# The opening of a one-core convolution and scan kernel: load order, the bias of the output, and the request for the second step's input

## The chip, the core and the metric

The kernel runs on one NeuronCore of a Trainium2 chip. The metric is the time of one execution on the device in microseconds; lower is better. PE is the matmul engine, PEld its weight loads, DVE the vector engine, ACT the scalar engine, POOL GpSimd, and SP the engine that issues nearly all DMAs. SBUF is the on-chip memory, PSUM the accumulator memory of PE with eight banks.

## The reference

The input x has the shape (4, 128, 96, 96) in fp32. Each image is normalised in 32 groups of four channels, and read as four sequences of 9216 positions: by rows, by columns, and both backwards. Each sequence goes through one block, and the four results are joined by one more matrix:

```python
t = grouped1x1(gn(x), in_proj_w, in_proj_b, 4)        # 128 -> 512 channels
u, gate = t[:, :256], t[:, 256:]
u = depthwise_conv5(silu(u), dw_w)
s, a = ssm_in(u), 0.999 + 0.0009 * sigmoid(delta(u))
h = linear_scan(a, tanh(b(u)) * s)                    # h[l] = a[l] h[l-1] + b[l] s[l]
u = u + ssm_out(tanh(c(u)) * h + d * s)
y_dir = out_proj(grouped1x1(u * sigmoid(gate), mix_w, mix_b, 4))
out = x + fuse_w @ concat(y_1 .. y_4) + fuse_b
```

`out_proj`, `mix` and `fuse` are linear with nothing between them. They can be multiplied into one matrix for each direction, `w_fin`, and one bias, `b_fin`, which is the same for all positions: the sum over the four directions d of `fuse_d (out_proj mix_b + out_proj_b)`, plus `fuse_b`.

## The kernel before

A sequence is cut into steps of 1536 positions (16 lines of the image). A position has one of R = 4 residues modulo four, so a step holds 4 x 384 positions; a *pair* is one step at one residue, for two sequences (s = 0 and s = 1) at once. For each pair the kernel runs, in this order: the *front* (`in_proj` from `x_in`, then `silu`), the depthwise convolution (half of the channels on PE as `conv` and `conv_less`, half as five taps, the first on ACT in L649 and four on DVE in L651, the last of which writes `u`), the projections `proj`, the scan, and, six pairs later, the gate, the output matmuls and the sum into `acc`. `pair(t)` computes the front of pair t + 4. Order on every engine is written out by hand from `start()` on; the opening before it is ordered by the framework's scheduler. In both kernels each engine runs its own instructions in order.

The opening has two threads.

- **Statistics.** `load_x` brings the whole first image into `acc` (4.7 MB, eight DMAs, one to four chunks of 384 positions each) and DVE runs one `bn_stats` for each of 24 chunks (L282). `stats_finish` then makes the normalised input weights `wn` and their bias `bnorm`: L184 on DVE, a small matmul L187 on PE, DVE, L199 on PE, DVE and ACT, L226 on DVE (which reads `main`), L235 on PE.
- **Weights.** `small`, `fuse` and `main` are loaded by ACT (L275). From `fuse`, PE makes `w_of` (eight matmuls, L364) and from that the final weights (eight, L371), with ACT copying each result. Twelve one-column matmuls (L379) add up the bias. Then `stay_busy` (L286) runs matmuls whose results nobody uses: four of 512 columns at once, and one of 256 and one of 512 columns inside the statistics' chain.

SP issues the loads of x, then the first step's `x_in` (L253) and gate inputs (L268). The program has eight semaphores for these DMAs in rotation, so that a DMA is issued only when the one eight before it has landed.

`start()` then runs the four residues of step 0: `burst(0, g)` (the matmuls for the first 32 of each sequence's 64 own rows of `x_in`), the silus of them, `burst(1, g)` for the second 32 rows, and after each of those `after_front(0, g)`, which asks for the next step's x: rows 64s+32 to 64s+64 of residue g each time, and rows 64s to 64s+32 of all residues when g is 3. Those rows may be overwritten once their bursts have read them. `pair(0)` follows. Its `proj` calls the front of step 1 (`front(4)`) between its own two halves; the first half reads `u` of the convolution on PE, the second `u` of the taps. `front(4)` uses PSUM banks 5, 4, 2 and 3, and `conv(2)` of the next pair uses 4 and 5. L632 and L634 are ACT's copies of the convolution's result into `u`; L683, L684 and L689 are ACT's reads of `proj`.

```python
def after_front(step, g):
    for s in range(2):
        load_front(step + 1, s, slice(64 * s + 32, 64 * s + 64), slice(g, g + 1))
    if g == R - 1:
        for s in range(2):
            load_front(step + 1, s, slice(64 * s, 64 * s + 32), slice(0, R))
```

Of the kernel before, what the change touches and what calls it, by code (L numbers as in the profile page):

```python
# [50 lines left out]
HID, MH, K = 256, 32, 5  # L51
# [5 lines left out]
R = 4  # L57
# [10 lines left out]
def conv_preact_kernel(  # L68
# [9 lines left out]
    nc = tc.nc  # L78

    wp = ctx.enter_context(tc.tile_pool(name="weights", bufs=1))  # L80
# [48 lines left out]
    def bank(i):  # L129
        return psum[:, i, :]  # L130

    def mm(o, col, lhsT, rhs, start, stop):
        r = slice(32 * col, 32 * col + 32)
        nc.tensor.matmul(o[r, : rhs.shape[-1]], lhsT, rhs, start=start, stop=stop,  # L134
                         skip_group_check=True)
# [35 lines left out]
    def stats_of(b):  # L171
        if b not in stats:
            stats[b] = sp.tile([P, NSC, 6], F32, tag="bn", name=f"bn_{b}")
        return stats[b]
# [71 lines left out]
    def fresh(step):  # L246

        return step * UB < NU and step % NS < NS // 2

    def load_front(step, s, r, q):  # L250
        if fresh(step):
            un = units[step * UB + s]
            nc.sync.dma_start(  # L253
                x_in[s][r, q, :], xs[un["b"], un["lay"], r, q, bass.ds(un["st"] * N, N + 1)]
            )
# [14 lines left out]
                xs[un["b"], un["lay"], half(1 - un["s"]), q, bass.ds(un["st"] * N, N + 1)],  # L270
            )

    def load(src, name, pool=wp):
        t = pool.tile(list(src.shape), F32, tag=name, name=name)
        nc.scalar.dma_start(t, src)  # L275
        return t

    def load_x(chunks):
        for c, n in chunks:
            nc.sync.dma_start(accf[:, bass.ds(c * SC, n * SC)], xr[b0, :, bass.ds(c * SC, n * SC)])  # L280
            for e in range(c, c + n):
                nc.vector.bn_stats(stats_of(b0)[:, e, :], accf[:, bass.ts(e, SC)])  # L282

    def stay_busy(n):
        if n:
            nc.tensor.matmul(  # L286
                bank(free[0] ^ 1)[:, :n], w_fin[:, 0, 0, :],
                w_fin.rearrange("p d j c -> p (d j c)")[:, :n], start=True, stop=True,
                skip_group_check=True,
            )  # L290
# [8 lines left out]
    pp = prep.__enter__()  # L299
    load_x([(0, 1), (1, 2), (3, 3)])  # L300
    w_small = load(small, "small")
    load_x([(6, 4)])
    w_out_fuse = load(fuse, "fuse", pp)
    load_x([(10, 4)])
    w_main = load(main, "main")
    load_x([(14, 4), (18, 4), (22, 2)])
    for s in range(2):
        load_front(0, s, half(s), slice(0, R))
    for i in range(UB):
# [4 lines left out]
    d_sb, b_mix, b_out, b_fuse = (w_small[:, a:b] for a, b in ((79, 80), (80, 82), (82, 83), (83, 84)))  # L314
    w_out = w_out_fuse[:, 0:HID]
    w_fuse = w_out_fuse[:, HID : HID + 4 * P].rearrange("p (d c) -> p d c", d=4)
    w_mix = w_out_fuse[:, HID + 4 * P :].rearrange("p (j c) -> p j c", j=2)
    w_in, w_proj = (
        w_main[:, bass.ts(e, HID)].rearrange("p (j c) -> p j c", j=2) for e in range(2)
    )  # L320
    w_so = w_main[:, bass.ts(2, HID)]

    nc.vector.tensor_scalar_mul(b_proj[64:P, 0:1], b_proj[64:P, 0:1], 0.5)
    nc.vector.tensor_scalar_mul(
        w_proj[:, :, 2 * MH : 3 * MH], w_proj[:, :, 2 * MH : 3 * MH], 0.5
    )


    def less_of(p):
# [30 lines left out]
    w_of = pp.tile([P, 4, 2, P], F32, name="w_of")  # L360
# [12 lines left out]
            )  # L373
            nc.scalar.mul(w_fin[:, d, j, :], pt[:, :P], 0.5)
    pb = bank(0)
    terms = [(w_of[:, d, j, :], b_mix[:, j : j + 1]) for d in range(4) for j in range(2)]
    terms += [(w_fuse[:, d, :], b_out) for d in range(4)]
    for i, (lhsT, rhs) in enumerate(terms):
        nc.tensor.matmul(  # L379
            pb[:, 0:1], lhsT, rhs, start=(i == 0), stop=(i == len(terms) - 1)  # L380
        )
    nc.scalar.activation(b_fin, pb[:, 0:1], AF.Identity, bias=b_fuse)
    for _ in range(4):
        stay_busy(512)
    prep.__exit__(None, None, None)

    wk = ctx.enter_context(tc.tile_pool(name="work", bufs=2))
# [64 lines left out]
    def edges(step, g, j, engine):  # L452
        sil = sils[step]
        if j == 0:
            for s in range(2):
                engine.memset(sil[64 * s : 64 * s + 64, s, 0, g, 0:1], 0.0)
        elif g < 2:
            engine.memset(sil[:, :, 1, g, 0:1], 0.0)

    def after_front(step, g):  # L460
        for s in range(2):
            load_front(step + 1, s, slice(64 * s + 32, 64 * s + 64), slice(g, g + 1))
        if g == R - 1:
            for s in range(2):
                load_front(step + 1, s, slice(64 * s, 64 * s + 32), slice(0, R))
        if step % NS < NS // 2 - 1:
            to_keep.append((step, g))
        if step > 1:
            keep_silu(1)
# [3 lines left out]
    def keep_silu(n):  # L473
        for step, g in to_keep[:n]:
            nc.sync.dma_start(kept_sil[step // NS % 2][step % NS][g], sils[step][:, :, :, g, :])
        del to_keep[:n]
# [9 lines left out]
    def in_proj(step, g, s, j, bk):  # L486
        wn = stats[units[step * UB]["b"]][0]
        r = slice(64 * s + 32 * j, 64 * s + 32 * j + 32)
        for c in range(4):
            m, q = (c, g) if j else (g, R - 1 - c if s else c)  # L490
            mm(bank(bk), c, wn[r, s, 32 * m : 32 * m + 32], x_in[s][r, q, :], True, True)

    def silu(step, g, s, j, bk):
        bn = stats[units[step * UB]["b"]][1]
        nc.scalar.activation(  # L495
            sils[step][:, s, j, g, :],
            bank(bk)[:, : N + 1],
            AF.Silu,
            bias=bn[:, 1:2] if j else bn[:, 4 + g : 5 + g],
        )  # L500
# [112 lines left out]
    def conv(i, banks):  # L613

        step, p = units[i]["step"], units[i]["p"]
        sil, k, b0 = blocks(step), less_of(p), min(banks)
        for s in range(2):
            for g in range(4):
                mm(bank(b0 + s), g, band[:, s, p, g, :], columns(step, sil[s][:, g, :], 1 - k),
                   True, False)  # L620

    def conv_less(i, banks):
        step, p = units[i]["step"], units[i]["p"]
        sil, k, b0 = blocks(step), less_of(p), min(banks)
        for g in range(4):
            for s in range(2):
                r = less_rows(s, p)
                mm(bank(b0 + s), g, less[r, p, g, :], columns(step, sil[s][r, g, :], k),
                   False, True)
        if banks == PROJ:  # L630
            for s in range(2):
                nc.scalar.copy(us[i][:, s, 0, :], bank(b0 + s)[:, :N])  # L632
        else:
            nc.scalar.copy(us[i][:, :, 0, :], psum[:, b0 : b0 + 2, :N])  # L634

    def new_u(i):
        us[i] = wk.tile([P, 2, 2, N], F32, tag="u", bufs=LAG + 2, name=f"u_{units[i]['id']}")

    def taps(i, ks):

        un = units[i]
        step = un["step"]
        sil = sils[step][:, :, 1] if fresh(step) else sils[step][:, ::-1, 1, ::-1]
        part = psum[:, TAPS : TAPS + 2, :N]
        for k in ks:
            off, q = divmod(un["p"] + k, R)
            src = columns(step, sil[:, :, q, :], off)
            if k == 0:
                nc.scalar.activation(part, src, AF.Copy, scale=w_tap[:, 0:1])  # L649
            else:  # L650
                nc.vector.scalar_tensor_tensor(  # L651
                    us[i][:, :, 1, :] if k == K - 1 else part,
                    src,
                    w_tap[:, k : k + 1],
                    part,
                    ALU.mult,
                    ALU.add,
                )
# [130 lines left out]
    def head_banks(t):  # L789

        return PROJ if t % 2 or t >= LAG else FRONT[1::-1]
# [209 lines left out]
    def start():  # L1001
        pieces = stats_finish(b0)
        for wait in (0, 256, 512, 0, 0):
            next(pieces, None)
            stay_busy(wait)
        sils[0] = wk.tile([P, 2, 2, 4, N + 1], F32, tag="sil", name="sil_0")
        banks = ((2, 3), (4, 5), (6, 7), (0, 1)), ((2, 3), (4, 5), (2, 3), (4, 5))

        def burst(j, g):
            for s in range(2):  # L1010
                in_proj(0, g, s, j, banks[j][g][s])

        def silus(j, g):
            for s in range(2):
                silu(0, g, s, j, banks[j][g][s])
            edges(0, g, j, nc.vector)

        for g in range(R):
            burst(0, g)
        for g in range(R):  # L1020
            silus(0, g)
        new_u(0)
        for g in range(R):
            burst(1, g)
            silus(1, g)
            after_front(0, g)
            if g < 2:
                taps(0, (g,))
            if g == 1:
                conv(0, head_banks(0))  # L1030
                conv_less(0, head_banks(0))
        taps(0, (2, 3, 4))
# [89 lines left out]
```

## Time and profile before

| what | value |
|---|---|
| three runs | 1831.49, 1835.07 and 1840.69 us; median 1835.07 |
| the profiled execution | 1833.3 us, of which the span of its instructions is 1831.6 us |
| granted PE clock, mean of the span | 0.996 |
| PE busy | 1806.8 us (99%) |
| ACT, DVE, POOL busy | 1566.0 us (86%), 1448.8 us (79%), 1423.5 us (78%) |
| DMA | 321 MB, 175 GB/s on average |

The profile gives the start and the length of each instruction, what ended the idle time before it, and the landing of each DMA; times are counted from the start of the span. A matmul in fp32 stands in it as two passes, each a record, so that eight matmuls are "x16".

### The profile page before, as it was taken

What the parts mean: (1) busy time and instruction counts of PE and PEld (TensorE: products, weight loads), DVE (VectorE), ACT (ScalarE), POOL (GpSimd) and SP (SyncE); (2) the same over time, 40 slices, a digit from 0 to 9 for tenths busy, and PEclk for the clock granted to TensorE, in tenths of its full rate; (3) what the DMA queues carried; (4) which work ended last, traced back from release to release, by engine and by line L of the source; (5) the groups of instructions that cost most, each with busy time, mean ns of one, the idle gap of its engine ahead of it and who ended that gap; (6) DMA issues with size and microseconds to landing.
All of it is one profiled execution on the core that took longest, in us unless ns stands there. A gap on an engine that the chain in (4) does not pass through costs nothing.

```text
span 1831.6 us, 57282 instructions
## 1 busy us (share of the span) xinstructions
PE 1806.8 (99%) x24068; PEld 653.9 (36%) x24068; DVE 1448.8 (79%) x1451; ACT 1566.0 (86%) x2762; POOL 1423.5 (78%) x1469
## 2 busy tenths in 40 slices
PE   7999999999999999999999999999999999999998
PEld 4333333333333333333333333333333333333333
DVE  5888878877878888877778888877877778777886
ACT  4888888988888888888898888888888888888975
POOL 2487887778777888787877888787877788887785
PEclk8999999999999999999999999999999999999999
DMA  6755563444965566244696546443476634535434
GB/s 196 200 191 179 164 192 108 161 144 147 307 227 181 167 188 190 102 142 140 214 296 207 165 162 211 136 152 110 162 236 223 234 123 152 192 109 179 148 122 156
DMA packets 147825, 321.18 MB, mean 175 GB/s; under 512 B 14192, under 2 KB 115696, under 8 KB 147568
## 3 DMA queue, kind: packets, MB, share of 16 engines
q1 hardware_dynamic: 147136, 316.56, 53.1%
q8 instruction: 190, 3.11, 0.7%
q10 hardware_dynamic: 432, 0.96, 0.1%
q14 instruction: 67, 0.55, 0.1%
HBM read 185.21 MB, written 132.25 MB: 173 GB/s over the span
## 4 chain that ended last, share of the span: by engine, by line
PE 96%; ACT 2%; DMA 1%; DVE 1%; issue 0%; SPq 0%; POOL 0%; ACTq 0%; DVEq 0%; POOLq 0%
PE psum L134 82%; PE psum L520 8%; PE psum L514 5%; ACT sil L495 0%; DMA x_in<-in_xs 0%; DMA fuse<-in_fuse 0%; PE psum L286 0%; DVE u L600 0%; ACT t L701 0%; ACT t L689 0%; PE psum L364 0%; ACT psum L649 0%; DMA out<-acc 0%; ACT u L632 0%; DVE psum L651 0%
## 5 line engine op out<-in xcount | busy, mean ns | idle before, releaser
L651 DVE SCALAR_TENSOR_TENSOR psum<-sil,small,psum 128x768 f32<-128x768 f32 x576 | 588.9, 1022 | 33.2 <-ACT psum L649 7.4
L600 DVE SCALAR_TENSOR_TENSOR u<-gate,psum 128x768 f32<-128x768 f32 x376 | 349.6, 952 | 256.6 <-ACT gate L537 118.6
L134 PE MATMUL psum<-u,w_fin 128*32 128x384 f32 x6176 | 551.7, 487 | 0.2 <-ACT t L689 0.2
L134 PE MATMUL psum<-u,main 128*32 128x384 f32 x6144 | 536.4, 490 | 0.1
L770 POOL TENSOR_TENSOR acc<-ys,acc 128x384 f32<-128x384 f32 x374 | 412.2, 1122 | 33.3 <-ACT ys L751 9.1
L724 POOL TENSOR_TENSOR t<-t,t 64x384 f32<-64x384 f32 x191 | 234.9, 1230 | 158.4 <-PE psum L514 78.8
L134 PEld LDWEIGHTS psum<-u,w_fin 128*32 128x32 f32 x6176 | 189.1, 110 | 320.8 <-issue 218.7
L134 PEld LDWEIGHTS psum<-u,main 128*32 128x32 f32 x6144 | 181.6, 110 | 327.6 <-issue 199.1
L528 ACT COPY psum<-u 128x768 f32<-128x768 f32 x352 | 276.9, 800 | 20.7 <-DVE u L651 10.2
L691 POOL TENSOR_SCALAR t<-tm 64x384 f32<-64x384 f32 x191 | 177.0, 927 | 151.0 <-ACT tm L683 100.8
L134 PE MATMUL psum<-sil,band 128*32 128x384 f32 x3072 | 286.8, 489 | 3.1 <-ACT ys L753 3.1
L725 POOL TENSOR_TENSOR t<-t,t 64x384 f32<-64x384 f32 x191 | 246.4, 1290 | 15.0
L520 PE MATMUL psum<-t,main 32*128 32x384 f32 x1536 | 241.9, 513 | 3.3 <-ACT psum L528 2.6
L649 ACT ACTIVATE psum<-sil,small 128x768 f32<-128x768 f32 x192 | 174.1, 907 | 63.2 <-DVE u L600 53.7
L537 ACT ACTIVATE gate<-psum,bnorm 128x384 f32<-128x384 f32 x384 | 192.6, 582 | 28.9 <-PE psum L514 26.9
L692 POOL TENSOR_TENSOR t<-t,tm 64x384 f32<-64x384 f32 x192 | 195.0, 1016 | 15.4 <-ACT t L684 0.2
L651 DVE SCALAR_TENSOR_TENSOR u<-sil,small,psum 128x768 f32<-128x768 f32 x192 | 194.9, 1015 | 7.8
L495 ACT ACTIVATE sil<-psum,bnorm 128x385 f32<-128x385 f32 x384 | 191.7, 584 | 3.6 <-PE psum L134 1.4
L134 PE MATMUL psum<-sil,less 64*32 64x384 f32 x3072 | 168.2, 495 | 0.0
L514 PE MATMUL psum<-x_in,wn 32*128 32x384 f32 x768 | 162.0, 528 | 2.3 <-ACT u L632 1.2
L753 ACT COPY ys<-psum 128x384 f32<-128x384 f32 x281 | 129.9, 476 | 30.2 <-PE psum L134 29.2
L134 PEld LDWEIGHTS psum<-sil,band 128*32 128x32 f32 x3072 | 90.2, 109 | 175.6 <-issue 94.1
(92 smaller groups left out, 1500.3 us busy)
## 6 DMA issues: line engine op xcount, KB each, us to landing
sil<-sil SPq DMA_DIRECT2D x128, 770.0 KB, 6.7
kept<-gate SPq DMA_DIRECT2D x80, 768.0 KB, 3.7
gate<-kept SPq DMA_DIRECT2D x76, 768.0 KB, 5.2
x_in<-in_xs SPq DMA_DIRECT2D x192, 96.2 KB, 2.4
out<-acc SPq DMA_DIRECT2D x48, 384.0 KB, 8.0
acc<-in_xr SPq DMA_DIRECT2D x38, 384.0 KB, 6.9
xs<-in_xr SPq DMA_DIRECT2D x72, 192.0 KB, 4.7
x_in<-in_xs SPq DMA_DIRECT2D x184, 48.1 KB, 3.7
```

Of the source, the lines that this page charges most:

```text
L134: nc.tensor.matmul(o[r, : rhs.shape[-1]], lhsT, rhs, start=start, stop=stop, skip_group_check=True)
L495: nc.scalar.activation(sils[step][:, s, j, g, :], bank(bk)[:, : N + 1], AF.Silu, bias=bn[:, 1:2] if j else bn[:, 4 + g : 5 + g],)
L514: nc.tensor.matmul(bank(to)[:, :N], stats[un["b"]][0][r, s, :], x_in[s][r, q, off : off + N], start=True, stop=True)
L520: nc.tensor.matmul(bank(SSM + 2 * s + j)[:, :N], w_so[r, bass.ts(j, P)], z[r, :], start=bi not in seeded, stop=True, skip_group_check=True)
L528: nc.scalar.copy(psum[:, SSM + 2 * s : SSM + 2 * s + 2, :N], us[bi][:, s])
L537: nc.scalar.activation(gv[:, s, j, :], bank(to[2 * s + j])[:, :N], AF.Tanh, bias=bn[:, 2 + j : 3 + j], scale=0.5,)
L600: nc.vector.scalar_tensor_tensor(v, g, 1.0, pz, ALU.add, ALU.mult)
L651: nc.vector.scalar_tensor_tensor(us[i][:, :, 1, :] if k == K - 1 else part, src, w_tap[:, k : k + 1], part, ALU.mult, ALU.add,)
L692: nc.gpsimd.tensor_mul(ta[0:64, p, :], tb[0:64, :], tm[0:64, :])
L724: engine.tensor_mul(ta[0:64, p, :], tb[64:P, :], ta[64:P, p, :])
L725: engine.tensor_add(tb[0:64, :], ta[0:64, p, :], tb[0:64, :])
L770: adder.tensor_add(part, y, part)
```

## The change

It touches the opening alone, in five places.

1. `fuse` and `main` are loaded by SP and no longer by ACT: `fuse` behind the first ten chunks of x, `main` behind all of them.
2. The halving of a part of `w_proj` moves from the head of the program to a place in `start()` behind the statistics' chain. It is on DVE in both.
3. The bias of the output takes three matmuls: `w_of` and `w_fuse` are first summed over the four directions, by four adds on POOL that write into their first slices.
4. The four 512-column `stay_busy` matmuls ahead of the statistics' chain are left out.
5. For step 0, the rows 64s to 64s+32 of the next step's x are asked for right behind the four `burst(0, g)`, and no longer behind the last `after_front(0, 3)`. The later steps are as before.

```diff
-    def load(src, name, pool=wp):
+    def load(src, name, pool=wp, queue=nc.scalar):
         t = pool.tile(list(src.shape), F32, tag=name, name=name)
-        nc.scalar.dma_start(t, src)
+        queue.dma_start(t, src)
         return t
...
     load_x([(6, 4)])
-    w_out_fuse = load(fuse, "fuse", pp)
-    load_x([(10, 4)])
-    w_main = load(main, "main")
-    load_x([(14, 4), (18, 4), (22, 2)])
+    w_out_fuse = load(fuse, "fuse", pp, nc.sync)
+    load_x([(10, 4), (14, 4), (18, 4), (22, 2)])
+    w_main = load(main, "main", wp, nc.sync)
...
-    nc.vector.tensor_scalar_mul(
-        w_proj[:, :, 2 * MH : 3 * MH], w_proj[:, :, 2 * MH : 3 * MH], 0.5
-    )
...
     pb = bank(0)
-    terms = [(w_of[:, d, j, :], b_mix[:, j : j + 1]) for d in range(4) for j in range(2)]
-    terms += [(w_fuse[:, d, :], b_out) for d in range(4)]
+    for w in (w_of, w_fuse):
+        for e in (2, 1):
+            nc.gpsimd.tensor_add(w[:, 0:e], w[:, 0:e], w[:, e : 2 * e])
+    terms = [(w_of[:, 0, j, :], b_mix[:, j : j + 1]) for j in range(2)]
+    terms += [(w_fuse[:, 0, :], b_out)]
...
     nc.scalar.activation(b_fin, pb[:, 0:1], AF.Identity, bias=b_fuse)
-    for _ in range(4):
-        stay_busy(512)
...
-        if g == R - 1:
+        if g == R - 1 and step:
             for s in range(2):
                 load_front(step + 1, s, slice(64 * s, 64 * s + 32), slice(0, R))
...
         for wait in (0, 256, 512, 0, 0):
             next(pieces, None)
             stay_busy(wait)
+        nc.vector.tensor_scalar_mul(
+            w_proj[:, :, 2 * MH : 3 * MH], w_proj[:, :, 2 * MH : 3 * MH], 0.5
+        )
...
         for g in range(R):
             burst(0, g)
+        for s in range(2):
+            load_front(1, s, slice(64 * s, 64 * s + 32), slice(0, R))
         for g in range(R):
             silus(0, g)
```

## The prediction, made before the changed kernel ran

> **What bounds the kernel now.** I read the page first: PE is busy for 1806.8 us of a span of 1831.6 us, so nearly all of the time that an edit of the opening could give back lies where PE is not yet running without breaks. Then I read the chain of waits for the first 120 us, the timeline of the same stretch, and the busy time in windows of 2 us. The chain (start, length, what):
>
> ```profile
> 1.31 5.42 DMA fuse<-in_fuse
> ...
> 13.42 2.57 PE psum L379 x24
> 16.00 5.24 PE psum L286 x8
> 21.24 0.13 PE psum L187 x2
> ...
> 33.74 3.40 DMA x_in<-in_xs
> 37.14 0.14 issue
> 37.28 7.77 PE psum L134 x80
> 45.05 0.05 ACT u L632
> ```
>
> Two places stand out. Ahead of 21.24 the chain lies on filler matmuls (L286), not on data. At 33.74 it lies on the load of the second step's x. The timeline says how near the next limit is in the first place:
>
> ```profile
> 10.87 8.52 DVE L282 BATCH_NORM_STATS2 bn<-acc 128x6 f32<-128x384 f32 x18 [0.25 <-DMA acc<-in_xr]
> 15.86 5.38 PE L286 MATMUL psum<-w_fin 128*128 128x512 f32 x8
> 19.42 0.80 DVE L184 BATCH_NORM_AGGREGATE mv<-bn 128x2 f32<-128x144 f32 x1
> 21.07 0.28 PE L187 MATMUL psum<-mv,gmean 128*128 128x1 f32 x2
> ```
>
> DVE has the means ready at 20.22 (19.42 + 0.80), but PE comes to L187 only at 21.07: the fillers cost 0.85 us, and DVE with the arrival of x sets the rest. In the second place:
>
> ```profile
> 36.00 1.01 DVE L651 SCALAR_TENSOR_TENSOR u<-sil,small,psum 128x768 f32<-128x768 f32 x1
> 37.11 0.91 ACT L649 ACTIVATE psum<-sil,small 128x768 f32<-128x768 f32 x1 [2.38 <-DVE u L651]
> 38.84 2.00 ACT L495 ACTIVATE sil<-psum,bnorm 128x385 f32<-128x385 f32 x4 [0.83 <-PE psum L134]
> 41.22 1.01 DVE L651 SCALAR_TENSOR_TENSOR u<-sil,small,psum 128x768 f32<-128x768 f32 x1
> ```
>
> So x at 37.28 is a wait for PE, but ACT could not have started the second step's silus before 38.02 anyway (L649 stands ahead of them and waits for DVE). The windows show what the gap did besides (length, PE, weight loads, DVE, ACT, POOL, granted clock, DMA):
>
> ```profile
> 34.00:36.00 2.00, 0.47 (x8) 0.00 (x0) 1.86 (x3) 0.73 (x2) 0.00 (x0) 1.00 0.49 126
> 36.00:38.00 2.00, 0.72 (x24) 0.36 (x32) 1.01 (x1) 0.89 (x1) 0.00 (x0) 0.65 0.41 113
> 38.00:40.00 2.00, 2.00 (x36) 0.33 (x24) 1.92 (x2) 1.17 (x4) 0.00 (x0) 0.50 0.06 13
> 40.00:42.00 2.00, 2.00 (x20) 0.66 (x16) 1.93 (x3) 1.42 (x3) 0.32 (x1) 0.50 0.57 179
> ```
>
> The clock fell to half and stayed there until 43.41 (clock records of the trace), so PE paid double from 37.28 on.
>
> **What the skill says.** TensorE: Matmul & The Clock Gate, section "What's actually happening": the array runs at half clock until it has been busy for a free-running window of about 3.4 us and falls back after an idle one. The trace agrees: a 512-column pass takes 0.85 us before 19.52 and 0.43 after, and the records change at steps of 3.413 us (16.105, 19.519, 36.585, 43.412). DMA: Bandwidth & Descriptors, "Issuing engines are not separate DMA queues": loads issued by ACT and SP share the same engines. The trace agrees: fuse (ACT) and the second x chunk (SP) land together at 6.74 and 6.24, and the pipe keeps some 418 GB/s with one issuer or two. GPSIMD Engine Reference, "Elementwise — side-by-side cycle accounting": 2.6 cycles an element for a two-input add; the rows here (128x128 0.40 us, 128x384 about 1.1) are what I use.
>
> **Part 1, order of the loads.** From 10.84 to 16.50, 2.36 MB of x landed, 417 GB/s; cumulative bytes B then land at about 3.82 us + B/417. With x ahead of main, and fuse behind the first ten chunks, I get: x chunks 0–9 by 3.5, 5.3, 6.8 and 8.6 (before 3.53, 6.24, 8.84, 10.84); fuse 9.9 (before 6.74); then 11.8, 13.7, 15.6, 16.5 (before 12.74, 14.61, 16.50, 18.11); main 17.4 to 18.1. A DMA waits for the landing of the one eight before it; the eight ahead of each land at least 1 us before the pipe needs it, so I put this at nothing. x_in comes behind the same bytes, so it lands as before, 19.94 and 21.88. DVE takes 0.473 us a chunk: it now waits for chunk 10 until 11.8 and is then level with the pipe (1.89 against 1.88 us for four), so six chunks after 15.55 end at 18.45: 0.94 us earlier, which is main's 0.39 MB. Bounds 0.4 and 1.4. ACT issues two DMAs fewer, at no gain: it idles until 7.61. The half scaling of w_proj (0.36 us of DVE) moves behind L240, where DVE waits 0.99 us for a silu: nothing, and 0.36 us if that cover is gone. main is needed at L226, some 22 us: 4 us of cover.
>
> **Part 2, bias from three matmuls.** 24 passes of 0.112 us (2.57) become 6 (0.7 at full clock, 1.3 at half). POOL gets four adds, estimated from its rows at 2.5 ns an element: 0.72, 0.39, 1.35, 0.72. fuse lands at 9.9, L364 and L371 take 16 passes of 0.213 us each at half clock, to 16.9. The w_fuse adds run from 13.5; the w_of adds from 15.3, when the first half of L371 is done, to 17.4; bias 18.1 to 18.8. The means are ready at 18.45 + 0.83 = 19.28. It is hidden, with a cover of 0.5 to 1.2 us; without it (second half of L371 awaited, adds at double) L187 moves to 20.4, a loss of 1.1.
>
> **Part 3, four fillers gone.** L187 starts at 19.3 in place of 21.07: 1.75 us, part 1 included. Against it stands the clock, which the fillers raised at 19.52. PE now has a hole from about 17 to 19.3, shorter than a window. If the clock stays high, the first burst starts at 22.6 (24.33 before); x_in at 21.88 allows it. If it is low, the 512-column filler kept behind L199 takes 1.71 us and ends at about 23.0, so that L235 gains 0.75, the bursts start at 24.0, and a group takes 0.64 us against ACT's 0.48 per silu until the clock rises, one window later on average: in sum 0 to 0.3 gained. I take the mean of the two, 1.0 us; bounds -0.6 and +1.75.
>
> **Part 4, the second step's x.** Two issues of 0.64 us move on SP ahead of eight smaller ones (0.37 each). Their wait for PE ends with the first bursts, near 26.9, so it holds nobody back; the first of the eight, at 27.37, slips to about 28.2 and lands at 30, wanted at 34.5. The load lands near 31 instead of 37.14, after the last of the first bursts. In the times of before, with the burst's own shift apart: front(4)'s matmuls run from 34.75, when silu has freed banks 4 and 5, to 36.1; proj's second half waits for u until 37.05 (before 39.37); ACT's L649 stays at 37.11, silus 38.04 (before 38.84), tm, L684 and L689 end at 41.5 (before 43.3). conv(2) waits for banks 4 and 5, freed by the second silu at 39.0, and runs at full clock 39.05–40.35, conv_less to 41.1 (before 44.9). Next is the copy L632: 41.5 against 45.03, **3.5 us**; then L649 and the taps follow, as u (42.23) is done. If the clock falls all the same, conv_less ends at 43.0, 2.0 us. The window from 33.17 to 36.58 was busy for 1.3 us of 3.41 when the clock fell; with front(4) in it, it is for 2.6. So I count the high clock two to one, and take 3.0. Late next are DVE's taps and ACT. From 57.48 the third step's load has its old place and moves with the rest (PE waits 0.5 there). PE has no break after about 80 us, so what is gained at 45 reaches the end.
>
> **Sum.** 1.0 + 3.0 = 4.0 us. The profiled execution took 1833.3 us (span 1831.6), which gives 1829.3. It lies 1.8 us under the median of the three runs, 1835.07; from that median, **1831.0**. The instruction order after the opening is the same as before, so I see no steady cost.
>
> **The rivals.**
> - Both clocks stay high and x is wholly early: 1.75 + 3.5, with a little of the 0.5 us of the third step: -5.5, 1829.5. For it: PE's hole is shorter than a window. Against: windows are not aligned to it.
> - The u of DVE rules: PE gets x early, the clock falls all the same, and ACT gives only the 0.8 us by which its silus move; with 0.7 at the start, -1.5: 1833.5. For it: L649's wait for DVE at 37.11. Against: the copy L632 waited for PE.
> - **Slower:** the clock, without its four fillers, stays at half from the first burst to 40 us. From the bursts to the end of front(4) PE has some 30 steps of 0.32 us (16 of the bursts, 4 of conv, 2 of conv_less, 4 of proj, 4 of front), each 0.64 at half clock: 19.5 us from 24.0, so that proj's second half comes at 43.5, not at 39.37: +4.1, with nothing from part 4: 1839.2. It decides when two full windows after the first burst still show 0.5. Against it: the bursts themselves are dense.
> - It doesn't do what it says: fuse, behind ten chunks of x, delays the preparation and L187 to 20.4; -3: 1832.
>
> **How the numbers follow.** Likeliest case 0.50 (own range 1829.5–1833), rivals 0.17, 0.15, 0.13 and 0.05 in their order. A measurement of this kernel can tell about 0.5%, 9.2 us, from no change, and no case reaches that on either side; the three runs of one kernel spread over 9.2 us, so a median may. That gives faster 0.06, same 0.91, slower 0.03. The range goes past -5.5 by the spread of runs below, and ends with the slower case above: 1825.0 to 1839.0.
>
> **What would show it.** Right: bn ends near 18.4, L187 near 19.3, no wait of PE for x_in before 45 us, no record of half clock near 37–43, L632 near 41.0 (45.03 less 4.0). Wrong: L187 waits for POOL's adds; half clock beyond 30 us; DVE's last chunk at 19.4 again; a new wait for x_in at the first burst; or PE idle beyond 45 us for loads that now come too close to each other.

## The result: slower, by a third of a per cent

The changed kernel takes 1841.06 us (median of 14 runs, 1837.79 to 1844.75), the kernel before 1835.19 us in the same comparison. The ratio is 1.0031, with a 95% interval from 1.0017 to 1.0044: about 5.7 us slower (3.1 to 8.1). The profiled execution took 1839.98 us, with a span of 1838.0 us and a mean granted clock of 0.992 (before 1833.3, 1831.6 and 0.996).

The timeline of the opening after the change, statistics and weights (start, length, engine, line, output from input):

```profile
10.24 3.78 PE L360 MATMUL psum<-fuse 128*128 128x128 f32 x16 [10.24 <-DMA fuse<-in_fuse]
12.19 6.63 DVE L282 BATCH_NORM_STATS2 bn<-acc 128x6 f32<-128x384 f32 x14 [1.30 <-DMA acc<-in_xr]
17.99 0.61 PE L378 MATMUL psum<-small,w_of 128*128 128x1 f32 x4 [1.38 <-POOL w_of L374]
18.86 0.81 DVE L184 BATCH_NORM_AGGREGATE mv<-bn 128x2 f32<-128x144 f32 x1
19.81 0.56 PE L187 MATMUL psum<-mv,gmean 128*128 128x1 f32 x2 [0.99 <-DVE mv L184]
21.94 2.06 PE L286 MATMUL psum<-w_fin 128*128 128x512 f32 x2
24.57 6.99 PE L134 MATMUL psum<-x_in,wn 32*32 32x385 f32 x96
```

L187 starts 1.26 us earlier, as it should. Then the filler that is left takes 2.06 us instead of 1.10, and the first bursts start at 24.57, later than before (24.33), and take 6.99 us for what took 3.85. The same two lines before:

```profile
22.59 1.10 PE L286 MATMUL psum<-w_fin 128*128 128x512 f32 x2
24.33 3.85 PE L134 MATMUL psum<-x_in,wn 32*32 32x385 f32 x96
```

The windows show why (length, then PE, weight loads, DVE, ACT, POOL, granted clock, share of the DMA engines, GB/s). After:

```profile
20.00:24.00 4.00, 4.00 (x12) 2.56 (x12) 1.48 (x8) 1.66 (x3) 0.00 (x0) 0.50 1.01 216
24.00:28.00 4.00, 4.00 (x81) 1.99 (x90) 0.55 (x5) 1.65 (x5) 0.00 (x0) 0.50 0.14 38
28.00:32.00 4.00, 4.00 (x61) 1.28 (x47) 0.35 (x6) 3.54 (x8) 0.00 (x0) 0.50 0.10 21
32.00:36.00 4.00, 4.00 (x40) 0.84 (x40) 1.14 (x3) 2.04 (x4) 0.00 (x0) 0.50 0.50 131
36.00:40.00 4.00, 3.71 (x80) 0.92 (x64) 2.04 (x2) 2.64 (x5) 0.00 (x0) 0.99 0.22 49
```

Before:

```profile
24.00:28.00 4.00, 4.00 (x130) 2.80 (x129) 0.62 (x7) 3.40 (x8) 0.00 (x0) 1.00 0.02 4
28.00:32.00 4.00, 4.00 (x56) 1.03 (x56) 0.24 (x4) 3.84 (x8) 0.00 (x0) 1.00 0.23 53
```

After the change PE is busy throughout from 20 to 36 us and yet at half clock: the trace's clock records have 0.5 from 18.988 to 36.055, five windows of 3.413 us. Behind that, the request for the second step's x does its work: no wait for x before 45 us, and u of the taps is what PE waits for, as part 4 had it.

```profile
41.09 1.50 PE L134 MATMUL psum<-u,main 128*32 128x384 f32 x16 [1.35 <-DVE u L648]
45.46 0.86 ACT L629 COPY u<-psum 128x384 f32<-128x384 f32 x2
```

The copy into u (L629 here, L632 before) stands at 45.46, before at 45.03:

```profile
45.03 0.86 ACT L632 COPY u<-psum 128x384 f32<-128x384 f32 x2 [1.73 <-PE psum L134]
```

The deficit had been 4.05 us where the last four silus of the second bursts start (36.76 against 32.71); with the early x it is down to 0.4, against this profile of before, in which PE waited for x and the clock fell at 36.59. If nothing else happened, the kernel would be the same. But the chain of waits goes on like this (start, length, what):

```profile
50.18 9.05 DMA sil<-sil
59.23 0.02 issue
59.24 5.69 DMA x_in<-in_xs
64.94 0.14 issue
65.07 8.08 PE psum L134 x96
73.15 0.84 ACT u L629 x2
```

and before like this:

```profile
58.31 4.32 DMA x_in<-in_xs
62.63 0.14 issue
62.76 6.37 PE psum L134 x96
69.13 0.84 ACT u L632 x2
```

The x of the *third* step lies behind the stores of `sil` in SP's queue, which write results of the silu out for later use. PE now waits 2.19 us for it instead of 0.46; behind that hole the clock falls once more (0.5 from 66.775 to 70.188), and the same 96 passes take 8.08 us instead of 6.37. That adds 3.4 us, and from 73 us on the kernel is 4.0 us behind. Small steps in the body add 0.8, and the end of the program, at half clock for longer (6.8 us instead of 3.4 near 1815), the rest of the 6.4 us between the two spans. The two stores ahead of that x were issued 1.83 us later than before (49.52 against 47.69); 1.29 us of that is one DMA issue on SP, of a chunk `xs`, which took 1.70 us at 47.25 and 0.41 before, for no reason that the trace shows.

### The profile page after: what moved, and what is told of

Same layout as the page of the kernel before. It is cut to its first block, busy times and chain, and to the rows that moved or that the text cites. A ratio compares the mean times of both kernels' runs of the same rounds, so it can differ in the third digit from the quotient of the medians.

```text
span 1838.0 us, 57238 instructions
## 1 busy us (share of the span) xinstructions
PE 1806.0 (98%) x24042; PEld 652.6 (36%) x24042; DVE 1449.6 (79%) x1451; ACT 1566.2 (85%) x2762; POOL 1427.6 (78%) x1473
## 4 chain that ended last, share of the span: by engine, by line
PE 95%; ACT 2%; DMA 1%; DVE 1%; issue 0%; POOL 0%; SPq 0%; DVEq 0%; POOLq 0%; ACTq 0%
PE psum L134 81%; PE psum L517 8%; PE psum L511 5%; ACT sil L492 1%; DMA sil<-sil 0%; DMA acc<-in_xr 0%; DVE bn L282 0%; DMA x_in<-in_xs 0%; DVE psum L648 0%; ACT psum L646 0%; ACT t L698 0%; DVE u L597 0%; ACT u L629 0%; ACT tm L680 0%; ACT t L686 0%
```

## The experiments

Ratios are against the kernel before, run on the same chip in the same comparison, with their 95% intervals. Line numbers differ between kernels by a few. Two theories stood at first: the **clock theory** (leaving out the fillers lost the clock of the opening) and the **load theory** (the loads' order and the third step's x).

### e3: the fillers alone left out

```diff
 # kernel before
-    for _ in range(4):
-        stay_busy(512)
```

> The kernel before without the four fillers, and nothing else changed. Clock theory: half clock from about 19 to 36 us, first burst near 24, and 4 to 6 us slower than before, as the whole change. Load theory: no loss, 0 to 1 us faster than before, since L187 comes 0.85 us earlier.

Ratio 1.0017 (1.0007 to 1.0027), 3.1 us slower. The windows of this kernel:

```profile
24.00:28.00 4.00, 4.00 (x83) 1.99 (x90) 0.45 (x4) 1.66 (x5) 0.00 (x0) 0.50 0.02 4
28.00:32.00 4.00, 4.00 (x68) 1.34 (x55) 0.35 (x6) 3.54 (x8) 0.00 (x0) 0.50 0.11 22
```

Half clock from 14.55 to 35.03, with PE busy without a break from 19.88 to 38.37. The clock theory's mechanism holds, and a loss that the load theory doesn't have; it is a little under the range named. It isn't the opening's alone, though: in this profile the clock fell again from 41.86 to 48.69, behind the wait for the second step's x, and PE waited 2.6 us for the third step's x, with the loads in their old order.

### e1: fillers where they cost nothing

In the time in which PE waits for POOL's adds.

```diff
 # changed kernel
+    for _ in range(6):
+        nc.tensor.matmul(
+            bank(1)[:, :HID], w_out[:, :P], w_out, start=True, stop=True, skip_group_check=True
+        )
     pb = bank(0)
```

> The changed kernel with six 256-column filler matmuls on w_out between L367 and the bias matmuls, in the time in which PE waits for POOL's adds. Clock theory (the 6 us are the half clock of 19 to 36 us, which came from leaving out the fillers): the clock is full from about 16 to beyond 45 us, the first burst starts near 23 us, the copy into u that stood at 45.0 before stands near 40.5, and the kernel is 3 to 5 us faster than before. Load theory (the loss comes from the loads' new order and the wait for the third step's x near 60 us): the clock may rise, but PE still waits for x_in near 60 us and the kernel stays 3 us or more slower than before.

Ratio 0.9993 (0.9981 to 1.0005): no difference from before, and below the whole interval of the changed kernel. In the profiled execution the opening went as the clock theory had it: full clock from 16.45, and the ACT instruction behind the copy into u stood 4.5 us earlier than before. Then it was lost near 60 us. The waits of PE between 45 and 80 us:

```profile
PE psum L134 <- DMA x_in<-in_xs: 2.6, 2, 1.6
```

```profile
60.00:64.00 4.00, 3.07 (x40) 0.63 (x28) 3.90 (x4) 2.10 (x5) 0.00 (x0) 0.60 1.07 210
64.00:68.00 4.00, 4.00 (x32) 1.31 (x28) 2.88 (x3) 0.63 (x2) 0.31 (x1) 0.54 0.91 302
```

Two waits, of 1.6 and 0.9 us (2.6 together), and half clock from 60.8 to 67.7: the lead of 4.5 us had become a lag of 1.1 by 75 us. So neither theory alone was enough.

### e2: fillers back at their old place

```diff
 # changed kernel
     nc.scalar.activation(b_fin, pb[:, 0:1], AF.Identity, bias=b_fuse)
+    for _ in range(4):
+        stay_busy(512)
```

> The changed kernel with the four 512-column fillers put back at their old place, which here lies behind the late bias matmuls. Clock theory: they run at half clock from 18.8, 1.7 us each, so that L187 comes near 24.5 instead of 19.8; the clock then rises near 22.4, the first burst starts near 27.5, and what that costs is given back by the early x: within 1.5 us of before. Load theory: the late start adds to the loss, 8 us or more slower than before.

Ratio 0.9994 (0.9982 to 1.0007), as the clock theory said, and L187 at 24.49. The clock rose at 23.39, and the bursts behind it held it until 64.35. There it fell behind a wait of 2.2 us for the third step's x, as in the changed kernel.

### e4 and e10: the early request, alone and left out

e4 is the kernel before with nothing but the early request, e10 the changed kernel without it:

```diff
+        for s in range(2):
+            load_front(1, s, slice(64 * s, 64 * s + 32), slice(0, R))
...
-        if g == R - 1:
+        if g == R - 1 and step:
```

> The kernel before with the second step's rows asked for behind the first bursts, and nothing else changed. Clock theory: front(4) no longer waits near 37 us, no half clock at 37 to 43, the copy into u at 45.0 moves to about 41.5, and the kernel is 2 to 4 us faster than before. Load theory: what is gained at 45 us is lost near 60 us to the wait for the third step's x: within 0.5 us of before or slower.

> The changed kernel with the second step's rows asked for at their old place, behind the last of the second bursts. If the early request gives 2 us or more also at half clock, as part 4 of the prediction has it, the copy into u that stands at 46.4 in the changed kernel comes near 49 to 51, and the kernel is 2 to 4 us slower than the changed one, 1.0045 to 1.006 of the kernel before. If half clock takes the gain, it is within 1 us of the changed kernel, near 1.003.

e4: ratio 0.9977 (0.9966 to 0.9988), 4.2 us faster, the best of all kernels here. L649, behind the copy into u, stands at 41.82 (before 45.91), and the clock is full from 19.03:

```profile
41.82 0.91 ACT L649 ACTIVATE psum<-sil,small 128x768 f32<-128x768 f32 x1
```

Of the lead of 4.1 us 2.7 are left when PE goes on at 60.07 (before 62.76), behind a wait of 1.7 us for the third step's x. e10: ratio 1.0038 (1.0023 to 1.0053). L649 stands at 50.5 instead of 46.4, so the early request is worth 4.1 us there, a second half clock in e10 (41.10 to 47.92) included; but the interval overlaps that of the changed kernel (1.0017 to 1.0044), so that the difference in the whole time isn't measured.

### e5: the kernel before once more

> The kernel before, unchanged, profiled once more. If the short wait for the third step's x (0.5 us near 62.8) belongs to the order of the old kernel, it is 0.5 us again and the clock stays full from 43 us on. If it hangs on how fast the stores of sil happen to drain (9.1 us for the second and third of them in the first profile, 10 to 11 us in three of the four experiments), the wait is 1.5 to 2.5 us, and the clock may fall behind it.

1832.18 us, with a wait of 1.2 us for the third step's x where the first profile had 0.5, and no second fall of the clock:

```profile
36.00:40.00 4.00, 3.12 (x55) 1.09 (x59) 2.90 (x4) 3.12 (x6) 0.00 (x0) 1.00 0.21 49
```

The same code had 0.57 in this window in the first profile, and stood 3.0 us behind this execution at 46 us. So the fall at 37 us, which the prediction counted as the kernel's, belongs to some executions only. Where it doesn't come, the early request has less to give: L649 stands at 42.92 here, so that e4 (41.82) leads by 1.1 us and not by 4.1, and the spans of the two are 1830.3 and 1830.4. The 4.2 us of e4 are a difference of medians; how much of them is the spared fall of the clock isn't measured. The changed kernel (46.35) is 3.4 us behind this execution at that place.

### e11 and e6: one more store early

The changed kernel (e11), and the one with early fillers (e6), with the first two stores of `sil` behind `pair(0)`:

```diff
-        keep_silu((1, 2, 1, 0)[t] if t < R else 0)
+        keep_silu((2, 1, 1, 0)[t] if t < R else 0)
```

> The changed kernel, without fillers, with two stores of sil behind pair(0) in place of one. If its loss has two parts, the half clock of the opening (0.6 us at 63 us) and the wait for the third step's x with a second fall of the clock (3.4 us from 63 to 70), this takes the second alone away: half clock from 19 to 36 as before, no wait of over 0.5 us near 65, and 2 to 4 us faster than the changed kernel, 1.000 to 1.0015 of the kernel before. If the second part was chance in one profile, it stays near 1.003.

> The changed kernel with the six early fillers, and the first two stores of sil instead of one behind pair(0), so that 770 KB go out near 37 us in place of 43 us. Store theory (the 5 us that the early fillers gained at 45 us were lost again because the third step's x lies in the queue behind the stores, and PE's wait for it drops the clock): x_in lands 1.5 us or more earlier, PE waits under 0.5 us near 58 us, the clock stays full, and the kernel is 4 us or more faster than before (ratio near 0.997). Rival (the wait follows from the weights' new place on SP, not from the stores): the wait near 60 us stays at 1.5 us or more, ratio near 0.9993 again.

e11: ratio 1.0002 (0.9991 to 1.0013), against 1.0031 of the changed kernel. The opening was no better than there (half clock from 22.41 to 36.07, the copy into u at 46.11), and still the wait for the third step's x was gone. The first two stores now go out at 41.56. Of the three that the changed kernel issues from 49 us on, in front of that x (two at 49.52, one at 55.37), two are left. In e11:

```profile
41.56 1.27 SPq L472 DMA_DIRECT2D sil<-sil  x2
50.03 0.52 SPq L472 DMA_DIRECT2D sil<-sil  x1
```

In the changed kernel:

```profile
40.98 0.59 SPq L472 DMA_DIRECT2D sil<-sil  x1
49.52 1.24 SPq L472 DMA_DIRECT2D sil<-sil  x2
```

The chain of waits of e11 runs through PE without a break:

```profile
47.06 5.80 PE psum L134 x96
52.86 0.04 issue
52.90 16.80 PE psum L134 x256
69.70 0.84 ACT u L629 x2
```

```profile
64.00:68.00 4.00, 4.00 (x72) 1.45 (x63) 3.81 (x4) 4.00 (x8) 0.32 (x2) 1.00 1.11 248
```

So the order of the stores, by itself, brings the changed kernel back to the kernel before. The profiles agree: in the four kernels with two stores behind `pair(0)` (e6, e7, e9, e11) PE waits for no x between 45 and 80 us, in the nine without it does, for 0.5 us (first profile), 0.7 (e8), 1.2 (e5) and 1.7 to 2.9 (the changed kernel, e1 to e4, e10). Whether the place in the queue or the bandwidth that the stores take is what holds the x back was not told apart. In the changed kernel one of its requests also waited 0.3 us for a store to land, since the semaphores go round in eights. e6: ratio 0.9986 (0.9976 to 0.9996), 2.6 us faster, no wait near 60 either. Its profiled execution lost the clock nevertheless, from 22.16 to 35.82, with the same opening as e1, which had kept it.

### e7 and e9: stores with the early request, four and six fillers

e7 is e4 with the stores of e11; e9 is e7 with six fillers of 512 columns in place of four.

> The kernel before with the early request for the second step's x and two stores of sil behind pair(0). Store theory: the wait of 1.7 us near 60 us of the early request alone goes too, and the kernel is 5 us or more faster than before (ratio 0.9972 or less). Rival: as with the early request alone, ratio 0.9977.

> The kernel before with the early x, two stores of sil behind pair(0), and six fillers of 512 columns in place of four. Window theory (where the windows of 3.4 us fall differs from execution to execution; at full clock four fillers end near 18.1 and leave PE idle for 2 us ahead of L187, and a window with that hole drops the clock): no hole, L187 between 20 and 23, full clock from 23 us at the latest in each execution, and the times spread less, with a median of 3 to 5 us under the kernel before. Rival (the longer fillers delay L187 as often as they save the clock): same as with four, ratio 0.9983, or slower.

e7: ratio 0.9983 (0.9975 to 0.9992), no better than e4, though no wait near 60 us was left. Its profiled execution is a counterpart to e4 with the same opening: the clock was already full when the four fillers ran, so they were through early, and L187 found PE idle:

```profile
20.14 0.35 PE L187 MATMUL psum<-mv,gmean 128*128 128x1 f32 x2 [2.02 <-DVE mv L184]
```

The clock fell at 20.40 and came back at 34.05. In e4 the clock was at half while they ran (15.62 to 19.03), they lasted until L187 at 20.54, and the clock stayed full. e9 closes that hole, and its profile has full clock from 18.40, but L187 only at 22.02; ratio 0.9982 (0.9972 to 0.9991), spread 1829.0 to 1834.2 (e7 1828.7 to 1834.1). Six fillers gave nothing over four.

### e8: small fillers

```diff
 # e1
-            bank(1)[:, :HID], w_out[:, :P], w_out, start=True, stop=True, skip_group_check=True
+            bank(1)[0:32, :HID], w_out[0:32, 0:32], w_out[0:32, :], start=True, stop=True, skip_group_check=True
```

> The changed kernel with the six early fillers cut to 32 rows and 32 columns of the array (the same 256 columns of input, so the same PE time). If the clock follows the share of the array at work, these do not hold it: half clock again from about 19 to 36 us, copy into u near 46, and 3 to 6 us slower than the kernel before. If it follows PE's busy time alone, it stays full as with the large fillers, and the copy stands near 41.4.

Inconclusive. Ratio 1.0006 (0.9997 to 1.0015), overlapping e1. The clock fell at 22.53 and rose at 32.77, but e6 with the large fillers fell at 22.16, so that this profile doesn't tell small from large.

## Why the prediction was wrong

It said 1831.0 us, with a range of 1825.0 to 1839.0; the median is 1841.06. It also gave 0.91 to a time within 0.5% of before, and there the ratio lies; but every case that it listed lies there too, so that this says nothing for its mechanism.

- **Part 3 failed, in the term for the clock.** It had the clock rise "one window later on average", and so 0 to 0.3 us gained at half clock. The half clock lasted five windows in the changed kernel, six in e3. The first burst started at 24.57 (24.0 said for that case), and by the silus of the second bursts 4.05 us were lost. e3 has this edit alone: +3.1 us, later waits included, where the sum had -1.0 for parts 1 and 3. Dense bursts were taken to raise the clock; at full clock they hold it (e2, e4), and in none of these profiles did a window filled with them raise it. The prediction counted a window as busy when PE is busy in the profile. Its own profile spoke against that: PE was busy for all of 12.69 to 16.11, with one-column matmuls for 2.57 us of it, and at 16.11 the clock fell; the fillers then raised it at 19.52.
- **The slower rival was the right mechanism, with too little weight (0.13) and the wrong end.** Its point of decision came true, two windows behind the first burst at 0.5. But the clock rose at 36.06, before front(4), and the early x was worth its gain: proj's second half came at 41.09, not at 43.5. In e11, which has such an opening without the later wait, the whole time is that of before again. The range ended at 1839.0, though this case was put at 1839.2.
- **Part 4 was right on its own ground, and failed in its last step.** The request alone gives 4.2 us (2.2 to 6.2) for 3.0 said; L632's wait for PE is gone, and DVE's taps are late next. "The third step's load has its old place and moves with the rest (PE waits 0.5 there)" is the step that failed: in the changed kernel PE waits 2.19 us for it, and 1.7 to 2.9 in e1, e2, e3, e4 and e10, where it stands behind the same stores. As e3 and e10 wait without the early request, that request isn't the reason by itself; and with 0.5, 0.7 and 1.2 us in other executions of the same order, the wait differs from one to the next. e11 shows what the stores' place costs the changed kernel: 1.0031 down to 1.0002. So "what is gained at 45 reaches the end" was wrong as well.
- **Part 1 did not hold beyond one profile.** Statistics ended at 18.83, 0.56 us earlier than before and not 0.94: fuse landed at 10.20 (9.9 said) and x_in at 21.13 and 22.91, over 1 us later than before. Nobody waited for that x_in. But over all the profiles the new order of the loads gains nothing: in the seven that have it the last `bn_stats` ends between 18.82 and 20.28 (median 19.32), in the six with the old order between 18.90 and 19.38 (median 19.06). The eleventh chunk of x, behind fuse, comes at 12.19 to 13.41 (11.8 said), DVE stands idle until then, and the 14 chunks from there take at least 6.6 us. That order alone was not run.
- **Part 2 held.** POOL's adds took 1.26 and 2.06 us (1.11 and 2.07 said), PE waited for them for 1.38 us until 17.99, and L187 did not wait for the bias.
- **The ground under part 4 was one execution.** The fall of the clock at 37 us was read as a property of the kernel; e5 shows the same code without it, behind a wait that was even longer (2.92 us, 2.81 in the first profile).

Parts of the loss can't be added up from single changes: early fillers take the changed kernel from 1.0031 to 0.9993, stores to 1.0002, both to 0.9986. How much of the remaining spread belongs to the place of the clock's windows was not measured.

## What to carry to other kernels

Filler matmuls ahead of a short chain may be what raises the clock and keeps it for the next 17 us (19.52 to 36.59 in the first profile): before they go, look in the windows at what will raise the clock in their place, and count dense work of a kind that was never seen to raise it as none. A profile's busy time doesn't answer that. When a stage is pulled forward, follow the next load in its queue to what stands ahead of it there; here, in the profile of the changed kernel, the wait for the third step's x and the fall of the clock behind it took back 3.4 us. And profile both kernels more than once before counting a fall of the clock, or half a microsecond of loading, as their own.

## What the hardware showed that was not expected

- **Bursts that hold a full clock did not raise a half one.** Bursts of matmuls with 32 rows and 32 columns kept a full clock: in e1 they fill 3.13 us of the window from 23.28 to 26.69, in e9 3.21 us of that from 25.23 to 28.64. At half clock nine windows were filled with them but for 0.1 us at most, in seven kernels (the changed one, e3, e6, e7, e8, e10, e11), and none raised the clock. These are the two of e3, and the one behind them, in which it rose:

```profile
24.79:28.21 3.42, 3.42 (x53) 1.40 (x53) 0.51 (x5) 1.76 (x4) 0.00 (x0) 0.50 0.02 5
28.21:31.62 3.41, 3.41 (x60) 1.01 (x46) 0.29 (x5) 2.96 (x7) 0.00 (x0) 0.50 0.07 14
31.62:35.03 3.41, 3.41 (x33) 0.76 (x32) 0.81 (x3) 2.33 (x4) 0.00 (x0) 0.50 0.22 49
```

The matmuls in them:

```profile
24.66 6.96 PE L134 MATMUL psum<-x_in,wn 32*32 32x385 f32 x96
31.56 2.79 PE L134 MATMUL psum<-sil,band 128*32 128x384 f32 x16
34.28 1.21 PE L134 MATMUL psum<-sil,less 64*32 64x384 f32 x16
```

In all seven it rose at the end of the first window in which the convolution's matmuls, on 128 and 64 rows, took 1.87 us or more (1.87 in e8, 1.88 in e10, 3.1 in the changed kernel); with 1.53 us of them in e6 and 1.09 in the changed kernel it stayed at half. That the rows are the reason is not shown: e8 did not settle it, and a window at full clock also holds nearly twice as many passes of the bursts (96 passes took 3.85 us before, 6.99 after).
- **A hole shorter than a window can drop the clock, or not.** The Trainium skill, TensorE: Matmul & The Clock Gate, "HAM oscillation — how this bites in real kernels", has it fall when a gap crosses a window of 3.4 us. Here 2.02 us (e7) and 2.19 us (changed kernel) sufficed. One of 1.7 us in e4 did not drop it, nor did one of 2.92 us in e5, while one of 2.81 us in the first profile, with the same code as e5, did. What differs between those two is the place of the hole in the free-running windows: PE was busy for 1.30 us of the one that ended with the fall (33.17 to 36.59), and for 1.41 us of the one without (32.55 to 35.96), with 2.50 us in the next. Busy time alone doesn't sort all cases: the changed kernel's clock fell behind a window with 1.70 us, 1.46 of it bursts.
- **More filler speed, less clock.** At full clock four fillers ended at 18.12, 2.02 us before L187 could start, and the clock fell (e7); at half clock the same four, begun at 15.32, lasted until L187 at 20.54 and it rose (e4).
